# A two-layer decoder on one core: layer 0's self-attention stepped by two head pairs instead of one

## The chip, the cores and the metric

The kernel runs on one core of a Trainium2 chip, in one launch. A core has a matrix engine (TensorE, PE in the profile; its weight loads are shown apart as PEld), a vector engine (VectorE, DVE), a scalar engine (ScalarE, ACT), a general engine (GpSimd, POOL) and a queue engine for transfers (SyncE, SP). Each takes its own instructions in order, and they wait for one another by semaphores. TensorE writes to PSUM, which here is cut into eight tiles of 128 partitions by 512 float32 numbers, called banks below; the other operands lie in SBUF. The metric is the device time of one execution in microseconds, median of several executions.

## The reference, cut to what matters

The whole is a decoder of two layers over 16 sequences of 256 tokens with 128 features. The change lies in the first of six blocks, layer 0's self-attention: 16 heads of 64, a linear bias by distance, a causal mask, softmax. The blocks after it in layer 0 are a cross attention with a gate and a mixture of experts.

```python
def _L0_attn_ref(x, Wq, Wk, Wv, Wo, bo):
    q = (x @ Wq).reshape(b, n, H, DH)
    k = (x @ Wk).reshape(b, n, H, DH)
    v = (x @ Wv).reshape(b, n, H, DH)
    scores = jnp.einsum('bihd,bjhd->bhij', q, k) * scale + bias[None]
    scores = jnp.where(causal[None, None], scores, jnp.float32(-1e+30))
    attn = jax.nn.softmax(scores, axis=-1)
    out = jnp.einsum('bhij,bjhd->bihd', attn, v).reshape(b, n, H * DH)
    return out @ Wo + bo
...
x = x + _L0_attn_ref(_layernorm(x, axis=-1), ...)
x = x + _L0_xattn_ref(_layernorm(x, axis=-1), ctx_1024, ...)
x = x + _L0_ffn_ref(_layernorm(x, axis=-1), ...)
```

## The kernel before

**Units and stages.** The stage works on 128 units: a unit is a sequence `b` (16) and a pair of heads `pair` (8). A unit passes through these functions, each with its line in the profile:

- `scores` (L450): four matmuls, each head with 64 rows of the array, so that two heads run side by side; a head's causal scores are 128 and 256 columns wide, in a PSUM bank of its own (pool `ps_s`, four banks).
- `greatest` (L463, VectorE): adds the bias from a table, writes the scores to SBUF and keeps the row's extreme; two instructions a head.
- `exponentials` (L475, ScalarE): two a head, with the row sums.
- `scaled` (L484 a reciprocal on VectorE, L486 two products on GpSimd): divides by the sums.
- `flip` (L497, TensorE): three 128x128 transposes a head, in a bank of pool `ps_m`; `flipped` (L502, VectorE) copies them to SBUF.
- `values` (L512, TensorE): four matmuls, each with 64 columns of the array, into one tile of pool `ps_o` (one bank); `values_out` (L524, ScalarE) copies it to SBUF.

Besides these the stage has the projections: `qk_mm` (L395) and `qk_out` (L406, ScalarE) for two units at a time, `v_mm` (L412) and `v_out` (L421, VectorE), `y_mm` (L427) and `y_out` (L435) for the output of a sequence, and `turn` (L131) with `turned` (L385) for the normed input of a chunk of two sequences. All of them, like the transposes, take their banks in turn from the three of `ps_m`: a tile waits until the tile three before it has been read.

**The step.** A loop runs 134 steps; the order of TensorE, VectorE and ScalarE is that of the program, written out by hand, while GpSimd's and SyncE's order is left to the scheduler. At step i, scores are made for unit i, `greatest` and `exponentials` for unit i-1, `scaled` for unit i-2, `flip` for unit i-4 and `values` for unit i-5. On TensorE a step is: projections, scores, values, transposes, side pieces.

**Side pieces.** While the attention of later sequences runs, the cross attention, the norm and the router of earlier chunks are done in small pieces: `front_pieces(c)` is a list for chunk c of 512 tokens, and `plan` puts its k-th piece into step 16c+22+k. A piece has a part for TensorE, placed after the transposes, and a part for the others, placed last in the step. Those that the prediction speaks of: `root` (three small GpSimd instructions, L346 and L348), `p_centred` and `p_centred2` (a small VectorE instruction, then four on ScalarE, L365), `mm_turn` and `mm_turn2` (four transposes of the outcome, L131), `p_first` and `p_second` (the router's choice: some 18 small VectorE instructions), `mm_gate` (L689, L696; eight matmuls into two banks) with `p_gate` (L705, two tanh on ScalarE), and `p_put` (L790: two indirect DMAs issued by GpSimd, four times a chunk). The pieces of chunks 6 and 7 that are left over at the end run in the mixture of experts, one for each of its tiles.

```python
                for mm, _, _ in pieces:
                    mm()
                if at(0):
                    scores(at(0))
                if at(5):
                    values(at(5))
                if at(4):
                    flip(at(4), 0)
                    flip(at(4), 1)
                for mm, _ in more:
                    if mm:
                        mm()
```

The functions that the change touches, and what calls them:

Of the kernel before, what the change touches and what calls it, by code (L numbers as in the profile page):

```python
# [15 lines left out]
F32 = mybir.dt.float32  # L16
# [6 lines left out]
P = 128  # L23
B, N, D = 16, 256, 128
# [3 lines left out]
NCHUNK = T // CH  # L28
# [7 lines left out]
EARLY_C = 6  # L36
# [26 lines left out]
def kernel(ctx: ExitStack, tc: tile.TileContext, a: dict, out: bass.AP):  # L63
    nc = tc.nc
# [173 lines left out]
    with ExitStack() as ph:  # L238
        DH = 64
        NPAIR = H // 2  # L240
# [102 lines left out]
        def root(c, what, scale=1.0, shift=LN_EPS):  # L343

            ve = small.tile([P, TPC], F32, tag="ln_ve0", name=f"ve_{what}_{c}", bufs=2)
            nc.gpsimd.tensor_scalar(ve, lnv[what, c][:, :, 1], scale, shift, ALU.mult, ALU.add)  # L346
            rstd = small.tile([P, TPC], F32, tag="ln_rstdf", name=f"rstd_{what}_{c}", bufs=3)
            nc.gpsimd.tensor_tensor(rstd, ve, nhalf, ALU.pow)  # L348
            lnv["r", what, c] = rstd
# [153 lines left out]

        def values(u):
            b, pair = u
            po = o_of[u] = ps_o.tile([P, N], F32, tag="o", name=f"o0_{b}_{pair}")
            v = vals[b, pair // 4]
            for jt, c0 in ((0, 0), (1, P)):
                for h in (2 * pair, 2 * pair + 1):
                    rows = slice((h % 2) * DH, (h % 2 + 1) * DH)  # L510
                    pT = pT_of[b, h]
                    nc.tensor.matmul(  # L512
                        po[rows, c0:N], v[:, jt, h % 8 * DH : (h % 8 + 1) * DH],
                        pT[:, 0:N] if jt == 0 else pT[:, N:],
                        start=(jt == 0), stop=(jt == 1),
                    )
            for h in (2 * pair, 2 * pair + 1):
                del pT_of[b, h]

        def values_out(u):  # L520
            b, pair = u
            if pair == 0:
                oT[b] = qkvp.tile([P, NPAIR, N], F32, tag="oT", name=f"oT0_{b}", bufs=1)
            nc.scalar.copy(oT[b][:, pair, :], o_of.pop(u))  # L524

# [66 lines left out]
        def front_pieces(c):  # L594
# [239 lines left out]
            def p_sdown():  # L834
                nc.vector.tensor_tensor(x[c], x[c], g.pop("sy"), ALU.add)

            first_part = [
                (None, lambda: stats(c, 0, "x0")),
                (None, lambda: stats(c, 2, "x0")),
                (None, lambda: root(c, "x0")),  # L840
                (None, p_centred),
                (mm_turn, p_turned),
                (mm_scores, p_leaky),
# [9 lines left out]
                (None, lambda: stats(c, 0, "f0")),  # L853
                (None, lambda: stats(c, 2, "f0")),
                (None, p_root2),
                (None, p_centred2),
                (mm_turn2, p_turned2),
                (mm_logits, p_logits),
# [132 lines left out]
        with tc.manual_schedule(engines=ordered):  # L991
            for t0 in (0, 2):
                stats(0, t0)
            normed(0, nc.vector)
            bias_strips()
            biased(0)
            turn(0)
            turned(0)
            for g in range(2):
                for which in range(2):  # L1000
                    qk_mm(g, which)
                    qk_out(g, which)
            front_constants()

            units = [(b, p) for b in range(B) for p in range(NPAIR)]
            n = len(units)
            side = {}  # L1010

            def plan(first, pieces):
                for k, piece in enumerate(pieces):
                    side.setdefault(first + k, []).append(piece)

            plan(17, [(lambda h=h: ctx_turn(h), lambda h=h: ctx_turned(h)) for h in range(2)])
            for c in range(NCHUNK):
                first_step = 16 * c + 22
                plan(first_step, front_pieces(c))
                if c == EARLY_C - 1:  # L1020
                    plan(first_step + 24, early_pieces())
                if c == NCHUNK - 1:
                    plan(first_step + 25, late_pieces())
            steps = 8 * (B - 1) + 14
            for i in range(steps):
                b, p = divmod(i, NPAIR)

                def at(lag):
                    return units[i - lag] if 0 <= i - lag < n else None

                pieces = []
                if i + 4 < n:
                    key = ((i + 4) // 2, i % 2)
                    pieces.append((lambda: qk_mm(*key), None, lambda: qk_out(*key)))
                if b < B and p in (2, 3, 6, 7):
                    vkey = (b, p // 4, p % 2)
                    pieces.append((lambda: v_mm(*vkey), lambda: v_out(*vkey), None))
                if p == 5 and 1 <= b <= B:
                    pieces.append((lambda: y_mm(b - 1), lambda: y_out(b - 1), None))
                if p == 7 and b % 2 == 0 and b // 2 + 1 < NCHUNK:  # L1040
                    c = b // 2 + 1
                    pieces.append((lambda: turn(c), None, lambda: turned(c)))
                more = side.get(i, [])

                for mm, _, _ in pieces:
                    mm()
                if at(0):
                    scores(at(0))
                if at(5):
                    values(at(5))  # L1050
                if at(4):
                    flip(at(4), 0)
                    flip(at(4), 1)
                for mm, _ in more:
                    if mm:
                        mm()

                if at(1):
                    greatest(at(1), 0)
                if at(2):  # L1060
                    scaled(at(2), 0)
                for _, out_v, _ in pieces:
                    if out_v:
                        out_v()
                if at(2):
                    scaled(at(2), 1)
                if at(1):
                    greatest(at(1), 1)
                if at(4):
                    flipped(at(4), 0)  # L1070
                    flipped(at(4), 1)
                if b % 2 == 0 and b // 2 + 1 < NCHUNK:
                    if p in (1, 3):
                        stats(b // 2 + 1, p - 1)
                    elif p == 4:
                        normed(b // 2 + 1)
                    elif p == 6:
                        biased(b // 2 + 1)

                if at(1):  # L1080
                    exponentials(at(1), 0)
                for _, _, out_a in pieces:
                    if out_a:
                        out_a()
                if at(1):
                    exponentials(at(1), 1)
                if at(5):
                    values_out(at(5))
                for _, post in more:
                    post()  # L1090


    pending = []
# [1049 lines left out]
```

## Time and profile before

| | us |
|---|---|
| median of 3 runs | 1545.54 (1542.36 to 1545.73) |
| the profiled execution, its own time | 1542.13 |
| its span in the profile | 1540.4 |
| first scores of layer 0's self-attention start | 18.3 |
| last scores start | 625.3 |
| first expert tile's transposes start | 652.9 |

The span is the time between the first and the last instruction of the program in the profile. The stage that the change touches takes the first 653 us of it. From then on the mixture of experts and layer 1 follow, whose code is not touched. The profile names a group of instructions by line, engine, operation, output and inputs with the tile of the array for matmuls (64*128 is 64 rows by 128 columns), the shape, the count, the busy time and the mean, and the idle time of the engine in front of them with what ended it.

### The profile page before, as it was taken

To read this page: it belongs to the slowest core of one execution; us is meant where nothing else is said; L and a number is where in the kernel's file an instruction comes from. 1 tells how busy PE (TensorE), PEld (TensorE's weight loads), DVE (VectorE), ACT (ScalarE), POOL (GpSimd) and SP (SyncE) were. 2 spreads that over 40 slices of the span, in tenths; PEclk is the share of its full clock that TensorE was granted. 3 is DMA by queue.
4 is the path that set the end of the run, shared out by engine and by line. 5 is a ranking of instruction groups with operands and counts; after the bars stand their busy time and mean duration, and the time that the engine had idled before them with its cause. 6 is when DMAs were issued, how large, how long until landed. Compare 5 with 4: busy or idle time off the path is not lost.

```text
span 1540.4 us, 34885 instructions
## 1 busy us (share of the span) xinstructions
PE 1460.9 (95%) x11569; PEld 1066.0 (69%) x11569; DVE 1175.1 (76%) x4620; ACT 970.7 (63%) x2619; POOL 664.8 (43%) x1102
## 2 busy tenths in 40 slices
PE   7999999999999999899999899999999996899987
PEld 4676666666666666589999777777777663565564
DVE  6666666667676767687878679999999977888873
ACT  5666565656565656354333378888888874667762
POOL 7354646464747464554533311111111006657642
PEclk9999999999999999999999989999999997999999
DMA  7760000000000000468777200000000000112122
GB/s 219 247 204 1 1 14 3 9 8 5 12 1 15 2 15 1 133 181 242 222 233 235 98 15 8 15 16 8 15 1 2 2 1 1 29 42 64 36 59 53
DMA packets 76321, 95.01 MB, mean 62 GB/s; under 512 B 15936, under 2 KB 59200, under 8 KB 76144
## 3 DMA queue, kind: packets, MB, share of 16 engines
q1 hardware_dynamic: 61312, 45.59, 10.9%
q10 hardware_dynamic: 10512, 38.28, 7.8%
q0 software_dynamic: 4320, 8.92, 1.7%
q8 instruction: 94, 1.54, 0.4%
q14 instruction: 83, 0.68, 0.2%
HBM read 64.11 MB, written 28.65 MB: 60 GB/s over the span
## 4 chain that ended last, share of the span: by engine, by line
PE 80%; DVE 13%; ACT 4%; issue 2%; DMA 1%; POOL 1%; POOLq 0%; DVEq 0%; SPq 0%; ACTq 0%
PE t L1587 7%; PE pqk L395 7%; PE s L450 6%; PE o L512 6%; PE t L497 5%; PE s L1555 5%; PE g L1298 4%; PE y L427 4%; PE u L1298 4%; PE y L1316 4%; PE o L1602 4%; PE pv L412 3%; PE pqk L1468 3%; DVE p L1566 2%; PE yf L2012 2%
## 5 line engine op out<-in xcount | busy, mean ns | idle before, releaser
L475 ACT ACTIVATE p<-p,nm 128x128 f32<-128x128 f32 (+1 forms) x512 | 227.6, 446 | 183.7 <-DVE nm L463 168.3
L486 POOL TENSOR_SCALAR p<-p,rs 128x128 f32<-128x128 f32 (+1 forms) x512 | 212.4, 431 | 188.8 <-DVE rs L484 160.8
L1577 ACT ACTIVATE p<-p,nm 128x256 f32<-128x256 f32 x512 | 225.9, 509 | 38.3 <-DVE nm L1566 35.9
L502 DVE COPY pT<-t 128x384 f32<-128x384 f32 x256 | 130.8, 552 | 101.8 <-PE t L497 101.8
L1566 DVE CUSTOM_DVE_ANT_0 p<-s,strip 128x256 f32<-128x256 f32 x512 | 188.0, 419 | 18.2 <-PE s L1555 16.0
L463 DVE CUSTOM_DVE_ANT_0 p<-s,strip 128x128 f32<-128x128 f32 (+1 forms) x512 | 158.0, 346 | 1.6 <-PE s L450 1.6
L1587 PEld LDWEIGHTS t<-ident,p 128*128 128x128 f32 x1024 | 111.2, 142 | 48.6 <-issue 13.0
L1587 PE MATMUL t<-ident,p 128*128 128x128 f32 x1024 | 141.5, 282 | 1.2 <-DVE pT L1595 1.2
L1433 POOL TENSOR_SCALAR ve_a<-mv_a 128x2 f32<-128x2 f32 x16 | 3.7, 229 | 267.8 <-DVE mv_a L1428 267.7
L1326 POOL DMA_INDIRECT rows_out<-yr,to x71 | 68.5, 964 | 116.2 <-DVE yr L1325 107.8
L450 PE MATMUL s<-k,q 64*128 64x128 f32 (+1 forms) x1024 | 118.5, 350 | 0.0
L512 PE MATMUL o<-pT,v 128*64 128x256 f32 (+1 forms) x1024 | 112.3, 339 | 0.8 <-DVE pT L502 0.8
L497 PE MATMUL t<-ident,p 128*128 128x128 f32 x768 | 112.9, 282 | 0.2 <-ACT k L406 0.2
L450 PEld LDWEIGHTS s<-k,q 64*128 64x128 f32 x1024 | 67.1, 186 | 62.5 <-issue 56.6
L512 PEld LDWEIGHTS o<-pT,v 128*64 128x64 f32 x1024 | 62.7, 136 | 61.4 <-issue 25.2
L497 PEld LDWEIGHTS t<-ident,p 128*128 128x128 f32 x768 | 81.6, 141 | 23.3 <-issue 16.1
L475 ACT ACTIVATION_READ_ACCUMULATOR p<-p,nm 128x1 f32 x512 | 96.6, 189 | 0.0
L1306 ACT ACTIVATE gs<-gs 128x512 f32<-128x512 f32 x71 | 44.7, 630 | 77.8 <-DVE gs L1305 65.6
L1595 DVE COPY pT<-t 128x512 f32<-128x512 f32 x128 | 87.8, 687 | 5.4 <-PE t L1587 2.3
L1555 PE MATMUL s<-k,q 32*128 32x256 f32 x1024 | 86.6, 410 | 1.4 <-DVE nm L1566 1.3
L421 DVE COPY v<-pv 128x512 f32<-128x512 f32 x64 | 43.9, 686 | 50.7 <-PE pv L412 50.7
L790 POOL DMA_INDIRECT rows_in<-xn,slot_in x64 | 63.7, 995 | 35.7 <-DVE nm L463 20.4
(338 smaller groups left out, 3482.1 us busy)
## 6 DMA issues: line engine op xcount, KB each, us to landing
gu<-in_L_ffn_gate_up_w ACTq DMA_DIRECT2D x71, 512.0 KB
rows_in<-zero SPq DMA_DIRECT2D x131, 130.0 KB
spread<-wrows SPq DMA_DIRECT2D x16, 512.0 KB
xr<-rows_in SPq DMA_DIRECT2D x71, 65.0 KB
y<-rows_out SPq DMA_DIRECT2D x16, 256.0 KB
x<-in_x SPq DMA_DIRECT2D x8, 256.0 KB
out_x<-yo SPq DMA_DIRECT2D x16, 128.0 KB
rows_out<-yr,to POOLq DMA_INDIRECT x71, 3.7
```

What stands on the lines that cost most here:

```text
L450: nc.tensor.matmul(ps_of[b, h][:, cols], q[rows, u2, iq], k[rows, u2, 0:nk], start=True, stop=True,)
L463: nc.vector.tensor_tensor_reduce(out=pr[:, cols], in0=ps[:, cols], in1=strip[:, h, P : 2 * P] if it == 0 else strip[:, h, :], scale=1.0, s ...
L475: nc.scalar.activation(pr[:, cols], pr[:, cols], AF.Exp, bias=nm[:, it : it + 1], scale=-1.0, accum_out=sm[:, it : it + 1],)
L486: nc.gpsimd.tensor_scalar(pr[:, cols], pr[:, cols], rs[:, it : it + 1], 1.0, ALU.mult, ALU.mult)
L497: nc.tensor.transpose(ps[:, cols], pr[:, cols], ident)
L502: nc.vector.tensor_copy(pT_of[b, h], tp_of.pop((b, h)))
L512: nc.tensor.matmul(po[rows, c0:N], v[:, jt, h % 8 * DH : (h % 8 + 1) * DH], pT[:, 0:N] if jt == 0 else pT[:, N:], start=(jt == 0), stop=(j ...
L1298: nc.tensor.matmul(ps[:, f, :], gu[:, lo + f * P : lo + (f + 1) * P], xT, start=True, stop=True,)
L1555: nc.tensor.matmul(ps_of[b, h][:, it, :], q[rows, g, it * P : (it + 1) * P], k[rows, g, :], start=True, stop=True,)
L1566: nc.vector.tensor_tensor_reduce(out=pr[:, it, :], in0=ps[:, it, :], in1=strip1[:, h, (1 - it) * P : (1 - it) * P + N], scale=1.0, scalar= ...
L1577: nc.scalar.activation(pr[:, it, :], pr[:, it, :], AF.Exp, bias=nm[:, it : it + 1], scale=-1.0)
L1587: nc.tensor.transpose(ps[:, jt, it * P : (it + 1) * P], pr[:, it, jt * P : (jt + 1) * P], ident,)
```

## The change

A step of the loop handles two units (four heads), and there are 67 steps instead of 134. At double step j the scores, `greatest` and `exponentials` are those of units 2j and 2j+1, `scaled` and `flip` those of the two units before, `values` those of the two before these. On TensorE the order is: scores of two units, both projections `qk_mm`, the first step's side pieces, the other projections, values of two units, transposes of four heads, the second step's side pieces. `values` writes the two units into one tile of a bank, and `values_out` copies both at once. On ScalarE the copies `qk_out` stand between the exponentials of the four heads. The lists of side pieces get one or two empty places for the earlier chunks.

```diff
         def values(u):
             b, pair = u
-            po = o_of[u] = ps_o.tile([P, N], F32, tag="o", name=f"o0_{b}_{pair}")
+            if pair % 2 == 0:
+                o_of[b, pair // 2] = ps_o.tile([P, 2, N], F32, tag="o", name=f"o0_{b}_{pair}")
+            po = o_of[b, pair // 2][:, pair % 2, :]
...
-        def values_out(u):
-            b, pair = u
-            if pair == 0:
+        def values_out(b, two):
+            if two == 0:
                 oT[b] = qkvp.tile([P, NPAIR, N], F32, tag="oT", name=f"oT0_{b}", bufs=1)
-            nc.scalar.copy(oT[b][:, pair, :], o_of.pop(u))
+            nc.scalar.copy(oT[b][:, 2 * two : 2 * two + 2, :], o_of.pop((b, two)))
...
+            wait = [], [(None, lambda: None)]
             first_part = [
...
                 (None, lambda: root(c, "x0")),
+                *wait[c <= EARLY_C],
                 (None, p_centred),
...
                 (None, p_root2),
+                *wait[c < EARLY_C - 1],
                 (None, p_centred2),
...
-                    plan(first_step + 24, early_pieces())
+                    plan(first_step + 25, early_pieces())
...
-            for i in range(steps):
-                b, p = divmod(i, NPAIR)
+            for j in range(steps // 2):
+                b, p = divmod(2 * j, NPAIR)
...
+                heads = [(u, k) for u in at(0) for k in range(2)]
+                before_them = [(u, k) for u in at(1) for k in range(2)]
...
+                more = [side.get(i, []) for i in (2 * j, 2 * j + 1)]
...
+                for u in at(0):
+                    scores(u)
+                for mm, _, _ in pieces[0:2]:
+                    mm()
+                run(0, 0)
+                for mm, _, _ in pieces[2:]:
+                    mm()
+                for u in at(2):
+                    values(u)
+
+                for u, k in before_them:
+                    scaled(u, k)
+                outs = [out for _, _, out in pieces if out]
+                for n in range(4):
+                    if heads:
+                        greatest(*heads[n])
+                        exponentials(*heads[n])
+                    if n < 3 and outs:
+                        outs.pop(0)()
+                run(0, 1)
                 for _, out_v, _ in pieces:
                     if out_v:
                         out_v()
...
+                for u in at(2)[0:1]:
+                    values_out(u[0], u[1] // 2)
+
+                for u, k in before_them:
+                    flip(u, k)
+                run(1, 0)
+                for u, k in before_them:
+                    flipped(u, k)
...
+                run(1, 1)
```

Here `run(k, 0)` issues the TensorE parts of the k-th of the double step's two lists of side pieces, and `run(k, 1)` their other parts.

## The prediction

> **What bounds the kernel now.** First the busy times, the whole span and then a stretch in the middle of the stage.
>
> ```profile
> PE 1460.9 (95%) x11569; PEld 1066.0 (69%) x11569; DVE 1175.1 (76%) x4620; ACT 970.7 (63%) x2619; POOL 664.8 (43%) x1102
> ```
>
> ```profile
> 300.00:400.00 100.00, 98.66 (x702) 67.18 (x702) 70.58 (x328) 61.12 (x220) 62.00 (x112) 1.00 0.04 12
> ```
>
> In that row (PE, PEld, DVE, ACT, POOL, then the granted clock) TensorE has 98.66 of 100 us at full clock and nobody else more than 71: the stage lasts as long as TensorE's stream, plus what it waits. Next, TensorE in order of time (start, length with overlap, what):
>
> ```profile
> 302.31 0.87 PE L497 MATMUL t<-ident,p 128*128 128x128 f32 x6
> 303.02 1.03 PE L395 MATMUL pqk<-xnT,wk 128*128 128x256 f32 x4
> 303.89 1.02 PE L412 MATMUL pv<-wv,xnT 128*128 128x512 f32 x2
> 304.84 0.93 PE L450 MATMUL s<-k,q 64*128 64x128 f32 x8
> 305.69 0.87 PE L512 MATMUL o<-pT,v 128*64 128x256 f32 x8
> 306.50 0.88 PE L497 MATMUL t<-ident,p 128*128 128x128 f32 x6
> 307.21 1.02 PE L805 MATMUL sg<-xT,sgu 128*128 128x512 f32 x2
> ...
> 332.08 0.87 PE L497 MATMUL t<-ident,p 128*128 128x128 f32 x6
> 333.60 1.13 PE L395 MATMUL pqk<-xnT,wk 128*128 128x256 f32 x4 [0.64 <-ACT q L406]
> ```
>
> ```profile
> 355.63 0.88 PE L497 MATMUL t<-ident,p 128*128 128x128 f32 x6
> 357.22 0.66 PE L131 MATMUL tp_f<-ident,xn 128*128 128x128 f32 x4 [0.71 <-ACT k L406]
> ```
>
> Starts minus starts give true costs. pqk to pv: 512 columns in 0.86, so 0.214 for 128. The scores stream 384 columns, two heads side by side, 0.64, but take 0.85; values 0.64, but 0.80; six transposes at a pitch of 0.109, 0.65, but 0.71; pv takes 0.95 ahead of the scores and 0.86 elsewhere. So each change of the array's tile (64*128, 128*64, 128*128) costs: 0.095 at the end of the group before, and at the start of the new one 0.107 (scores), 0.05 (values), 0.06 (transposes); a projection after a 64-row or 64-column group starts 0.1 late (1.06 against 0.96). Both waits above return every 16 units: 1.52 and 1.59 from transposes to the next group against 0.71, together 1.7 a period of 81.0 us (sg at 307.21 and at 388.2).
>
> Last the stage's tail, with GpSimd's and VectorE's rows:
>
> ```profile
> 630.01 0.88 PE L497 MATMUL t<-ident,p 128*128 128x128 f32 x6
> 633.98 2.07 PE L817 MATMUL su<-xT,sgu 128*128 128x512 f32 x2 [3.08 <-DVE rs L669]
> ...
> 643.68 0.88 PE L497 MATMUL t<-ident,p 128*128 128x128 f32 x6
> ```
>
> ```profile
> 633.09 0.96 POOL L790 DMA_INDIRECT rows_in<-xn,slot_in  x1 [0.30 <-issue]
> 634.09 3.65 POOL L486 TENSOR_SCALAR p<-p,rs 128x128 f32<-128x128 f32 x8
> ```
>
> ```profile
> 644.27 1.02 DVE L502 COPY pT<-t 128x384 f32<-128x384 f32 x2 [3.79 <-PE t L497]
> ```
>
> After 3 us idle TensorE runs slowly: su took 2.07 against 1.02, clock 0.60 from 634 to 638. GpSimd had been issuing DMAs (one per 1.27 us) ahead of the softmax products.
>
> **The change part by part.** *Fewer tile changes.* A unit has three now: into scores 0.095+0.107, into values 0.095+0.05, into transposes 0.095+0.06: 0.50, 1.01 for two. A double step has four: 0.20, 0.15, 0.16, and scores to projections 0.095+0.1: 0.70. That saves 0.31 x 64 = 19.8. Of the side pieces, two (cw and sp, 64 columns) now stand between transposes and scores, where a change is paid anyway: 0.2 each, 2 x 6 chunks = 2.4.
>
> *Two waits.* Both were for a projection's bank, whose copy (L406) stood behind long side work on ScalarE. Now the copies stand among the exponentials, ahead of it: 1.7 x 6 = 10.2 gone; 0 if other banks are late there instead, which the next items count.
>
> *The fourth head's bank.* Four heads are transposed in a row into three banks; the fourth waits until VectorE has copied the first. From the tail's rows: the copy starts 0.59 after the first transpose (644.27-643.68), lasts 0.55, and a matmul follows some 0.08 later: 1.24 after the first transpose, where without a wait it would be 1.04. 0.20 x 64 = 12.8; nothing hides it, because scores stand behind it in TensorE's queue. Bounds 0.17 and 0.25: 11 to 16. [...] Were every copy waited for, it would be 4 x 0.475, the copies' pitch, less 4 x 0.33 of transposes: 0.6 a double step, 38 in all; the rows show three banks running ahead, so I keep 0.20.
>
> *Shorter distance from softmax to transposes.* It was two steps (9 us); now GpSimd's products come in the same double step. A clock of one, from the first score: scores end at 1.5, projections at 3.3, values 1.43 later, so transposes start at 4.8 at the earliest, and later where pv, y or side matmuls stand before them. VectorE ends the last copies at 0.8, then four reciprocals; GpSimd needs 0.82 a head: 1.1 to 4.4. Hidden by 0.4 us or more, if GpSimd is free. ScalarE: first exponential at 1.35, 0.89 a head, 0.48 a projection copy, the first of them not before 2.65: ends at 6.3. Four kinds of double step, once per period each, miss this clock:
> - Two `root`s: the compiled order of GpSimd puts them (1.1 + 2 x 0.28) ahead of the products, after two pairs of statistics (0.81 each) on VectorE; the products run from 3.4 to 6.7, the last transposes want theirs by 6.05. 0.55.
> - Two centrings: 2 x 1.55 on ScalarE (four L365 took 1.55) from 6.3 to 9.4, and `mm_turn` wants the second at 8.6 (it had a whole step). 0.9.
> - `p_second`: 2.4 of small instructions on VectorE, then two v copies of 0.61, stand ahead of the copies L502; the v banks come free at 7.2 and 7.9, the second and third head want them at 6.9 and 7.6, and the first copy starts only then. 0.6.
> - The gate: four banks in a row; projections and tanh free them 0.13 and 0.22 late. 0.35.
>
> Sum 2.4 x 6 = 14.4. None of them has a row of its own before: bounds 0 (each piece hidden) and twice that, 29. I take the worked clocks.
>
> *Tail.* GpSimd's compiled order has all eight DMAs of chunk 5 (8 x 1.27 = 10.2) ahead of the last four heads' products. From the step of the last two units on: matmuls 21.5, end 33.2 us later, so 11.7 lost; before, from 621.4 to 652.3 with 23.5 of matmuls, 7.4 lost. +4.3, between -2 and +8.
>
> *At nothing:* the 512-column copy of values (one of some 0.57 for two of 0.36; ScalarE idles 39%); one piece of chunk 6 that moves into the experts' tiles (VectorE alone, under TensorE's stream); SyncE's queue keeps its order and its transfers end before they are wanted. Without that cover: 1 us at most.
>
> Sum: -19.8-2.4-10.2+12.8+14.4+4.3 = -0.9. On the profiled execution's 1542.13: 1541.2; on the median of the runs, 3.4 higher, 1544.6. I say 1543.
>
> **Rivals.** *The waits of the special steps are hidden* (ScalarE and VectorE come to them earlier than my clocks): without 14.4 and 4.3 the sum is -19.6, about 1524. For it: both have 30 to 39% idle. Against: their queues are in order and the late work stands ahead by the program. Chance 0.20.
>
> *GpSimd becomes late* (slower). Seven DMAs (8.9 us) stand between the products of two double steps, and in later chunks mix and norm (7 us) ahead of the next. By my clock products end 0.8 us before their transposes want them. If each GpSimd piece is 10% longer than its row, that cover is gone and two double steps a period lose some 2 us each: 24 more, about 1567. It decides from 0.8 us on. For it: this is the shortest cover in the stage, and the tail's rows show just such a queue. Against: 62 of 100 us busy. Chance 0.17.
>
> *It does nothing*: the order compiled for TensorE shows eight score matmuls in a row, so tile changes do go. Only if a change costs nothing beyond its first would the time stay. Chance 0.03.
>
> **How the numbers follow.** My case, that new waits eat the saving, has 0.60, its own range 1533 to 1556. With bounds: low -19.8-2.4-10.2+11+5+2 = -14, 1529; high -22.2-5+16+22+8 = +19, 1562. That alone would leave out both rivals, 0.37, so the low end goes on to take in the faster one: 1521 to 1562, with some 0.18 left out, most of it the slower rival. This kernel's measurement tells 0.3%, 4.6 us. My case splits 0.20, 0.18, 0.22; with the rivals faster 0.40, same 0.21, slower 0.39.
>
> **What would show it.** Eight scores at 1.48 and eight values at 1.43 confirm the tile changes; a wait of 0.2 for VectorE's copy (L502) in front of the fourth head's transposes in each double step; a period near 80.6; a wait of 5 us near the end. Wrong if the period is under 79 (hidden waits) or over 83, with TensorE waiting for GpSimd's L486.

## The result, and the profile after

The changed kernel takes 1544.50 us (median of 12 runs, 1539.05 to 1552.34), the kernel before 1544.93 us beside it (12 runs, 1539.49 to 1550.91): a ratio of 1.0002, with a 95% interval from 0.9986 to 1.0018. Measured again on another occasion the ratio is 1.0004 (0.9987 to 1.0022). There is no difference that this measurement can tell. The profiled execution took 1547.82 us, its span is 1546.1.

That is not because nothing happened. Cut into four parts by the starts of TensorE's rows, with the second traces of both kernels beside the first, in us:

| part | before | before_again | after | after_again |
|---|---|---|---|---|
| start to first scores | 18.30 | 18.71 | 17.31 | 16.91 |
| first scores to first expert transpose (`xTr`) | 634.65 | 634.77 | 629.72 | 629.48 |
| first to last expert transpose | 211.91 | 211.89 | 219.50 | 218.10 |
| from there to the end of the span | 675.56 | 677.79 | 679.58 | 678.16 |
| one period of 16 units (`sg` to `sg`) | 81.03 | 81.04 | 79.92 | 79.88 |

The attention stage became 4.9 to 5.3 us shorter; the experts' part, whose code was not touched, became 6.2 to 7.6 us longer. In these two pairs the first scores start 1.0 and 1.8 us earlier, but in the traces of the other double-step kernels below they start between 17.2 and 18.4, so no gain is shown there. The last part is 2.2 us longer in the mean of two traces, as much as the two traces of the kernel before differ.

In three of the four sets of experiments below the kernel before itself took 1566 to 1568 us instead of 1545, and every double-step kernel traced there shows a stall that no other trace shows (last section), so times are compared only within a set, and TensorE's rows only in stretches without the stall.

The busy times and the stretch in the middle of the stage, for the kernel after:

```profile
PE 1458.2 (94%) x11569; PEld 1087.6 (70%) x11569; DVE 1176.0 (76%) x4620; ACT 965.2 (62%) x2555; POOL 659.5 (43%) x1102
```

```profile
300.00:400.00 100.00, 98.33 (x705) 70.09 (x703) 72.51 (x346) 62.78 (x220) 57.84 (x107) 1.00 0.04 11
```

TensorE is still busy for 98 of 100 us at full clock: the stage is still as long as TensorE's stream. Both waits of before for projection banks are gone. This is the list of what TensorE waited for over four periods (line, what it waited for, us in total, times, longest), first before, then after:

```profile
PE tp_f L131 <- ACT k L406: 2.9, 4, 0.7
PE pqk L395 <- ACT q L406: 2.5, 4, 0.6
```

```profile
PE t L497 <- DVE v L421: 1.3, 4, 0.3
```

5.4 us of waits became 1.3, and the one that is left is the router's choice (`p_second`), whose `v` copy stands ahead on VectorE. TensorE in order of time, for the kernel after:

```profile
301.24 1.52 PE L514 MATMUL o<-pT,v 128*64 128x256 f32 x16
302.69 0.55 PE L497 MATMUL t<-ident,p 128*128 128x128 f32 x3
303.56 1.58 PE L497 MATMUL t<-ident,p 128*128 128x128 f32 x9 [0.32 <-DVE v L421]
...
305.56 1.58 PE L450 MATMUL s<-k,q 64*128 64x128 f32 x16
307.07 1.13 PE L395 MATMUL pqk<-xnT,wq 128*128 128x256 f32 x4
...
309.33 1.52 PE L514 MATMUL o<-pT,v 128*64 128x256 f32 x16
310.79 1.81 PE L497 MATMUL t<-ident,p 128*128 128x128 f32 x12
312.45 1.13 PE L806 MATMUL sg<-xT,sgu 128*128 128x512 f32 x2
```

Starts minus starts: eight scores take 1.51 (305.56 to 307.07) where two groups of four took 1.71, eight values 1.46 (309.33 to 310.79) where they took 1.60. Twelve transposes take 1.66 (310.79 to 312.45), and 1.74 where scores follow, where two groups of six took 1.42. The group is printed without a wait: the fourth head's pause, about a quarter of a microsecond, lies inside it, and only the instructions' own starts show it.

The stage's tail, TensorE and then GpSimd:

```profile
613.51 1.58 PE L450 MATMUL s<-k,q 64*128 64x128 f32 x16
...
620.74 1.58 PE L497 MATMUL t<-ident,p 128*128 128x128 f32 x9 [1.05 <-DVE v L421]
...
625.27 0.61 PE L664 MATMUL sm<-half_of,ex 128*128 128x2 f32 x4 [1.51 <-ACT ex L659]
...
630.73 3.55 PE L497 MATMUL t<-ident,p 128*128 128x128 f32 x12 [2.85 <-POOL p L486]
634.08 1.91 PE L818 MATMUL su<-xT,sgu 128*128 128x512 f32 x2
```

```profile
629.30 0.96 POOL L791 DMA_INDIRECT rows_in<-xn,slot_in  x1 [0.30 <-issue]
630.30 3.24 POOL L486 TENSOR_SCALAR p<-p,rs 128x128 f32<-128x128 f32 x8
```

The last transposes wait 2.85 us for GpSimd's products, which stand behind the last of the chunk's DMAs. With the waits of 1.51 and 1.05 and one of 0.34 that is 5.75 us, and the transposes at 630.73 run at half speed (clock 0.50 from 626.6 to 636.8).

The experts' part: what TensorE waits for, from the first to the last expert transpose, before and then after:

```profile
PE g L1298 <- ACT xTs L1270: 1.3, 3, 0.6
PE u L1298 <- DVE hT L1310: 1.1, 1, 1.1
PE xTr L1266 <- DVE x L435: 0.5, 1, 0.5
```

```profile
PE g L1311 <- ACT xTs L1283: 4.1, 5, 2.6
PE u L1311 <- DVE hT L1323: 1.7, 2, 1.1
PE sm L664 <- ACT ex L659: 1.2, 1, 1.2
...
```

2.9 us became 7.7 (the line left out is the 0.5 for `x` again, and one of 0.2 follows): 4.8 of the 7.6. Two places hold most of it. TensorE in order of time, first the rows of before, then those of after that hold both places:

```profile
684.07 1.06 PE L1298 MATMUL u<-xTs,gu 128*128 128x128 f32 x8
684.96 1.02 PE L805 MATMUL sg<-xT,sgu 128*128 128x512 f32 x2
685.82 0.51 PE L663 MATMUL sm<-half_of,ex 128*128 128x2 f32 x4
```

```profile
682.46 0.61 PE L664 MATMUL sm<-half_of,ex 128*128 128x2 f32 x4 [1.24 <-ACT ex L659]
685.85 1.02 PE L806 MATMUL sg<-xT,sgu 128*128 128x512 f32 x2
...
707.54 1.18 PE L1311 MATMUL g<-xTs,gu 128*128 128x128 f32 x8 [2.56 <-ACT xTs L1283]
708.53 1.89 PE L1311 MATMUL u<-xTs,gu 128*128 128x128 f32 x8
```

Before, chunk 6's `sg` stood in the same tile as chunk 7's `sm` and ahead of it: its microsecond covered the exponential that `sm` needs. With an empty place more in chunk 6's list, `sg` comes a tile later, and `sm` waits bare. The second place is the wait of 2.56 at 707.54, after which `u` takes 1.89 instead of 1.06: the clock was 0.51 from 708.5 to 711.9. On ScalarE the copy that it waits for stands behind an issue of expert weights, which itself waited, by the profile, for a transfer of layer 1's weights (`wq_u`) that SyncE had issued:

```profile
706.57 0.35 ACTq L1272 DMA_DIRECT2D gu<-in_L_ffn_gate_up_w  x1
707.02 0.46 ACT L1283 ACTIVATE xTs<-xTr,bet,gam 128x128 f32<-128x128 f32 x1 [5.28 <-DMA wq_u<-in_L_xattn_wq]
```

In the second trace of the changed kernel the sum of waits is 7.7 again, the longest 1.6, with no half clock here. So 4.8 of the 6.2 to 7.6 us are waits in both traces and about 1.7 (half of 3.4 us) are the clock in the first; some 1.2 are not accounted for.

### The profile page after: what moved, and what is told of

It reads as the page before. It is cut to its first block, busy times and chain, and to the rows that moved or that the text cites. A ratio compares the mean times of both kernels' runs of the same rounds, so it can differ in the third digit from the quotient of the medians.

```text
span 1546.1 us, 34991 instructions
## 1 busy us (share of the span) xinstructions
PE 1458.2 (94%) x11569; PEld 1087.6 (70%) x11569; DVE 1176.0 (76%) x4620; ACT 965.2 (62%) x2555; POOL 659.5 (43%) x1102
## 4 chain that ended last, share of the span: by engine, by line
PE 72%; DVE 14%; ACT 5%; issue 4%; POOL 3%; DMA 1%; ACTq 0%; POOLq 0%; SPq 0%; DVEq 0%
PE t L1600 8%; PE pqk L395 6%; PE s L1568 5%; PE s L450 5%; PE t L497 5%; PE o L514 4%; PE o L1615 4%; PE y L427 4%; PE g L1311 3%; PE y L1329 3%; PE u L1311 3%; PE pqk L1481 3%; PE pv L412 2%; PE yf L2025 2%; PE tx L1879 2%
## 5 line engine op out<-in xcount | busy, mean ns | idle before, releaser
L486 POOL TENSOR_SCALAR p<-p,rs 128x128 f32<-128x128 f32 (+1 forms) x512 | 209.2, 430 | 108.4 <-DVE rs L484 107.0
L502 DVE COPY pT<-t 128x384 f32<-128x384 f32 x256 | 125.7, 550 | 77.3 <-PE t L497 77.1
L463 DVE CUSTOM_DVE_ANT_0 p<-s,strip 128x128 f32<-128x128 f32 (+1 forms) x512 | 146.9, 352 | 11.3 <-PE s L450 9.8
L1600 PE MATMUL t<-ident,p 128*128 128x128 f32 x1024 | 142.4, 283 | 1.2 <-DVE pT L1608 1.2
L497 PE MATMUL t<-ident,p 128*128 128x128 f32 x768 | 115.9, 283 | 12.3 <-POOL p L486 3.2
L450 PE MATMUL s<-k,q 64*128 64x128 f32 (+1 forms) x1024 | 101.2, 337 | 0.0
L514 PE MATMUL o<-pT,v 128*64 128x256 f32 (+1 forms) x1024 | 97.8, 333 | 0.0
L1319 ACT ACTIVATE gs<-gs 128x512 f32<-128x512 f32 x71 | 44.7, 630 | 79.9 <-DVE gs L1318 66.8
L450 PEld LDWEIGHTS s<-k,q 64*128 64x128 f32 x1024 | 72.6, 187 | 14.4 <-issue 9.4
L1311 PE MATMUL g<-xTs,gu 128*128 128x128 f32 x568 | 75.7, 276 | 4.2 <-ACT xTs L1283 4.1
```

The source lines that it names most:

```text
L450: nc.tensor.matmul(ps_of[b, h][:, cols], q[rows, u2, iq], k[rows, u2, 0:nk], start=True, stop=True,)
L463: nc.vector.tensor_tensor_reduce(out=pr[:, cols], in0=ps[:, cols], in1=strip[:, h, P : 2 * P] if it == 0 else strip[:, h, :], scale=1.0, s ...
L486: nc.gpsimd.tensor_scalar(pr[:, cols], pr[:, cols], rs[:, it : it + 1], 1.0, ALU.mult, ALU.mult)
L497: nc.tensor.transpose(ps[:, cols], pr[:, cols], ident)
L502: nc.vector.tensor_copy(pT_of[b, h], tp_of.pop((b, h)))
L514: nc.tensor.matmul(po[rows, c0:N], v[:, jt, h % 8 * DH : (h % 8 + 1) * DH], pT[:, 0:N] if jt == 0 else pT[:, N:], start=(jt == 0), stop=(j ...
```

## The experiments

**Scores apart again (split_scores, split_again).** The cost of a tile change on its own: the scores of the two units with a projection between them, all else as in the changed kernel.

```diff
-                for u in at(0):
+                n_qk = 2 if 2 * j + 4 < len(units) else 0
+                for k, u in enumerate(at(0)):
                     scores(u)
-                for mm, _, _ in pieces[0:2]:
-                    mm()
+                    for mm, _, _ in pieces[k : min(k + 1, n_qk)]:
+                        mm()
                 run(0, 0)
-                for mm, _, _ in pieces[2:]:
+                for mm, _, _ in pieces[n_qk:]:
                     mm()
```

> The changed kernel, but with each unit's scores followed by one projection instead of both units' scores together. Theory 1 (the forecast's: every change of the array's tile costs TensorE time that nothing hides): two more changes per double step, scores to projection 0.095 and 0.1, projection to scores 0.095 and 0.107, 0.40 x 64 = 25 us more, 1570, ratio 1.017; two groups of eight scores at 0.85 instead of one of sixteen at 1.51. Theory 2 (the changes lie under other waits): within 5 us of 1544.5, since the wait for the fourth bank or for the softmax shrinks by as much.

Measured 1594.13 us against 1568.35 of the kernel before, ratio 1.0154 (1.0131 to 1.0178); with the stall in it, this says nothing of a tile change. It was run once more:

> The split of the scores once more, for a chip without the unnamed stall. Theory 1 (a change of the array's tile costs TensorE about 0.1 at each end and nothing hides it): two more changes per double step, 0.40 x 64 = 25 us over the changed kernel's 1544.8, 1570, ratio 1.016; the period rises from 79.9 by 3.2. Theory 2 (the changes lie under other waits): within 5 us of 1544.8.

1589.93 against 1566.16, 1.014 (1.010 to 1.0179), the stall again. The rows can be read all the same. TensorE in order of time, in the second run:

```profile
194.13 0.93 PE L450 MATMUL s<-k,q 64*128 64x128 f32 x8
194.98 1.13 PE L395 MATMUL pqk<-xnT,wq 128*128 128x256 f32 x4
196.04 0.93 PE L450 MATMUL s<-k,q 64*128 64x128 f32 x8
```

Four scores take 0.85 or 0.86 again and each projection behind them 1.06. Per period scores and `pqk` cost 13.69 + 16.32 where they cost 12.09 + 14.74: 3.19 more, 0.40 for each of eight double steps, as the prediction's prices say (two entries at 0.2). From the first scores to the fifth `y`, a stretch of 23 double steps with no stall, the split kernel takes 198.54 us and the changed one 191.29, 7.25 more: scores and `pqk` take 9.2 more, again 0.40 a double step, and `pv`, transposes and `tp_x` 1.9 less. Tile changes do cost what the rows of before showed.

**A fourth bank for the transposes (bank4).** The first of four heads takes its bank from the scores' pool.

```diff
-            ps = tp_of[b, h] = ps_m.tile([P, 3 * P], F32, tag="m", name=f"t0_{b}_{h}")
+            if h % 4 == 0:
+                ps = ps_s.tile([P, 4 * P], F32, tag="s", name=f"t0_{b}_{h}")[:, 0 : 3 * P]
+            else:
+                ps = ps_m.tile([P, 3 * P], F32, tag="m", name=f"t0_{b}_{h}")
+            tp_of[b, h] = ps
```

> The changed kernel, but the first of four heads is transposed into one of the four banks of the scores, so that the four heads have four banks. Theory 1 (the forecast's third term): in each double step the pitch before the fourth head's transposes is 0.36 instead of 0.11, with the one behind it 0.28 lost; it goes, 0.28 x 64 = 17.7 us less, 1527, ratio 0.989, and the sixteen-step transposes take 1.46. Theory 2 (VectorE's copies are the bound, so the wait only moves): the scores' fourth bank is now wanted before its copy (L502) has ended, TensorE waits there instead, less than 5 us come off, 1540 or more.

1586.93 against 1568.35, 1.0112 (1.0091 to 1.0132): the least of the four of this set, and all four have the stall. What the bank brings is read below, in the kernel that holds this edit and no stall.

**Chunk 6 without its empty place (slot6, slot6_again).** The edit takes back the part of the change that moved chunk 6's pieces one tile on in the experts.

```diff
-                *wait[c <= EARLY_C],
+                *wait[c < EARLY_C],
```

> The changed kernel, but chunk 6 without its empty slot, so that its last pieces keep their old place beside the experts' tiles. Theory 1 (giveback at the experts): in the changed kernel GpSimd issues chunk 6's eight put DMAs from 689.3 to 699.3 and two rows_out after them, so chunk 7's mix1 (L711) runs at 701.88 although its tanh ended at 695.63; VectorE (L716) then holds back xTs and TensorE waits 2.56 us at 707.5 and runs at half clock for some 4 us. One tile (3 us) earlier, mix1 follows its tanh at once, the wait and the slow clock go: 4 to 5 us less, 1540, ratio to before 0.997. Theory 2 (the difference between 647 and 712 is that of two executions): no wait goes, 1544.5, ratio 1.000.

1591.86 against 1568.35, 1.0145 (1.0122 to 1.0168), with the stall. Run again, without the stall:

> The changed kernel without chunk 6's empty slot, measured beside the changed kernel itself. Theory 1 (giveback at the experts): GpSimd's mix1 of chunk 7 (L711) follows its tanh at once, the wait of 2.56 us before a tile's g and the half clock behind it go, 4 to 5 us under the changed kernel in the same call. Theory 2 (the difference between 647 and 712 is that of two executions): the same as the changed kernel.

1545.20 against 1546.15, 0.9993 (0.9973 to 1.0013). The experts' part came down to 215.56 us, with neither the wait of 1.24 nor that at 707; but the stage went up to 632.51. (The expectations lay the wait at 707 to GpSimd's late `mix1`; in the rows of the changed kernel it is ScalarE's issue of weights, shown above, that ends it.) TensorE in order of time shows where:

```profile
598.48 0.66 PE L131 MATMUL tp_x<-ident,xn 128*128 128x128 f32 x4 [1.43 <-ACT q L406]
599.84 1.12 PE L412 MATMUL pv<-wv,xnT 128*128 128x512 f32 x2 [0.70 <-ACT k L406]
601.75 1.12 PE L412 MATMUL pv<-wv,xnT 128*128 128x512 f32 x2 [0.78 <-DVE v L421]
...
657.10 1.81 PE L1311 MATMUL g<-xTs,gu 128*128 128x128 f32 x8 [2.23 <-ACT xTs L1283]
```

Without the empty place chunk 6's first centring falls into the same double step as chunk 5's second, eight ScalarE instructions (1.65 + 1.64 us) in one go, and two banks wait behind the copies that stand after them, a third behind a `v` copy: 2.9 us, which is what the stage lost. The wait of 2.23 at 657.10 comes from GpSimd: a small mask for layer 1 is made there behind a memset of 3.51 us, and VectorE, in its compiled order, has the mask's reduction (L1163) ahead of the first tile's gate, behind which ScalarE's next copy for TensorE stands. GpSimd, then VectorE:

```profile
649.35 3.51 POOL L1148 MEMSET vbd<- 128x4096 f32 x1 [2.67 <-PE y L427]
```

```profile
654.57 0.18 DVE L1163 TENSOR_REDUCE rmask<-hmask 128x4 f32<-128x16 f32 x1 [4.01 <-DMA xr<-rows_in]
```

The place is a trade: 2.5 to 3.9 us won among the experts, 2.8 to 3.0 lost in the stage.

**The two kernels themselves again, and both edits together (before_again, after_again, bank4_slot6).** These belong to one set with slot6_again, in which the kernel before took 1546.15 (25 runs) and no trace has the stall.

> The kernel before, for a trace on the chip of this call. In the chip of the last call every kernel showed one stall per period that the earlier traces lack: ScalarE (or VectorE) waits up to 5.5 us for a releaser that the profile can't name, while GpSimd issues eight put DMAs, and TensorE then runs at half clock for 3 to 7 us. Theory 1 (the chip does it, to every kernel): a call on the same chip shows it here too, 1568; on another chip it is absent, 1545. Theory 2 (only the double steps provoke it): no such stall here on any chip.

> The changed kernel, beside the kernel before on the same chip. Theory 1 (the stall belongs to the chip): without it, period 79.9 and ratio 1.000; with it, period 87 and ratio 1.01 to 1.02. Theory 2 (the experiments' edits provoked it): period 79.9 on any chip.

> The run before, and with the first of four heads transposed into a bank of the scores. Theory 1 (the wait for the fourth bank, 0.28 x 64 = 17.7 us, goes): 17 us under the run before; the period falls by 2.2. Theory 2 (VectorE's copies are the bound, the wait only moves to the scores' fourth bank): less than 5 us.

The kernel before, again: 1544.90 (one run). The changed one: 1544.82, 1.0004 (0.9987 to 1.0022). Both edits together: 1538.30 us, ratio 0.9958 (0.9935 to 0.9981), 6.9 us under slot6_again: the only version here that is measurably faster than the kernel before (of its ten runs only the longest, 1543.84, lies above the shortest of the changed kernel's ten, 1543.56). Its stage takes 626.61 us (632.51 in slot6_again), its experts' part 215.44. TensorE in order of time, in two double steps of it:

```profile
331.97 1.53 PE L501 MATMUL t<-ident,p 128*128 128x128 f32 x12
333.43 1.58 PE L450 MATMUL s<-k,q 64*128 64x128 f32 x16
...
346.85 2.51 PE L501 MATMUL t<-ident,p 128*128 128x128 f32 x12
349.29 1.58 PE L450 MATMUL s<-k,q 64*128 64x128 f32 x16
```

Where scores follow, twelve transposes take 1.46 instead of 1.74: the 0.28 of the fourth head are gone. But the saving is only 5.9 us, not 0.28 x 64 = 17.9, and the period falls by 0.28 (79.91 to 79.63), not by 2.2: in a full period only two of the eight double steps gain the 0.28. Where another group that takes one of the three banks follows (`sg`, `sy`, `tp_f`), transposes to that group take the same 1.66 or 1.75 as without the further bank; ahead of `cw` they gain 0.08; ahead of `pos` they take 2.36 instead of 2.31, and in the double step of the roots, at 346.85, 2.44 instead of 2.17. 3.9 of the 5.9 us lie ahead of the first `sg` (at 228), where fewer side pieces stand. So the size of the pause was read rightly from the rows; what a further bank returns is a third of it over the stage, and an eighth in a full period. The experts' part starts 6.0 us earlier than in slot6_again and is as long (215.44 and 215.56), so it does not wait for something that comes at a fixed time.

**The v copies ahead of the router's choice (vout_first).**

```diff
-                run(0, 1)
+                own = any(mm for mm, _ in more[0])
+                if own:
+                    run(0, 1)
                 for _, out_v, _ in pieces:
                     if out_v:
                         out_v()
+                if not own:
+                    run(0, 1)
```

> The changed kernel, but with the v copies (L421) ahead of a side piece that has no matmul of its own (p_second). Theory 1 (the forecast's special step): the transposes of that double step take 1.74 instead of 2.30 from their start to the next group, 0.56 x 6 = 3.4 us less, 1541, ratio 0.998. Theory 2: p_second's 2.4 us now delay the copies L502 behind it or the positions' matmul, and the wait comes back there: 1544.5.

1590.58 against 1568.35, 1.0136 (1.0112 to 1.016), with the stall; and a miss in the rows too. TensorE, then VectorE:

```profile
223.74 1.20 PE L497 MATMUL t<-ident,p 128*128 128x128 f32 x9
226.09 0.52 PE L497 MATMUL t<-ident,p 128*128 128x128 f32 x3 [1.15 <-DVE pT L502]
```

```profile
225.40 1.94 DVE L502 COPY pT<-t 128x384 f32<-128x384 f32 x4
```

The copies now wait for `pv`, the router's small instructions begin only after them, and the copies of the transposes start at 225.40: the fourth head waits 1.15, and the group takes 2.72 us instead of 2.30. In this double step, whichever stands first on VectorE, the other is late.

**Chunk 6 kept in place without losing its empty place (realign), and the puts of chunk 5 later (late_puts_h).** realign joins two pieces of chunk 6's list, so that the empty place shifts nothing behind it:

```diff
-                (None, lambda: stats(c, 0, "f0")),
-                (None, lambda: stats(c, 2, "f0")),
+                *([
+                    (None, lambda: (stats(c, 0, "f0"), stats(c, 2, "f0"))),
+                ] if c == EARLY_C else [
+                    (None, lambda: stats(c, 0, "f0")),
+                    (None, lambda: stats(c, 2, "f0")),
+                ]),
```

> The changed kernel with chunk 6's empty slot kept, but its two pairs of second statistics in one piece, so that from there on its pieces keep their old place beside the experts' tiles. Theory 1 (in the changed kernel the shifted pieces cost the experts' part 6.2 to 7.6 us, of which a late rmask 0.7): the attention stage keeps its 629.5 us from first scores to first expert transpose, the experts' part falls from 218.1 or 219.5 to about 213, 5 to 6 us less, 1539, ratio 0.997. Theory 2 (any place of these pieces costs as much, as the run without the slot suggests, which gave back in the stage what it gained): 1545.

late_puts_h gives chunk 5 two empty places ahead of its puts, so that they stand behind the last products on GpSimd, and makes the mask among the constants at the start:

```diff
                 (None, p_second),
+                *wait[c == EARLY_C - 1],
+                *wait[c == EARLY_C - 1],
                 (mm_pos, p_pos),
...
-    hmask = lpool.tile([P, H], F32, tag="hmask", name="hmask")
```

> The changed kernel with chunk 5's token positions two slots later, so that its eight put DMAs stand behind the last four heads' products on GpSimd, and with the head masks built at the start. Theory 1 (the forecast's tail: products behind eight puts): the wait of 3.0 us before the last transposes, most of the 1.0 and 1.2 waits ahead of it and some 5 us lost to half clock behind them go, the first expert transpose comes at 640 instead of 646.4, 1539, ratio 0.996. Theory 2 (the puts then end at 634 and the rows that the experts fetch are late by as much): the first expert transpose waits for its rows, 1545 or more.

realign: 1584.49 against 1566.16, 1.0103 (1.0061 to 1.0145). late_puts_h: 1581.21, 1.0088 (1.0054 to 1.0122). Both have the stall, and their intervals overlap. In realign's trace the wait of `sm` among the experts is gone. It is there, 1.23 to 1.25 us long, in all seven traces of kernels in which chunk 6 is shifted, and in none of the five in which it is not (slot6, slot6_again, bank4_slot6, realign, combined), nor in the two of the kernel before: this much is shown. late_puts_h removed the wait of 2.85 before the last transposes (0.19 is left), but TensorE waits at the next place:

```profile
656.21 1.20 PE L497 MATMUL t<-ident,p 128*128 128x128 f32 x6 [0.19 <-DVE rs L678]
...
679.47 1.86 PE L1313 MATMUL g<-xTs,gu 128*128 128x128 f32 x7 [7.66 <-ACT xTs L1285]
```

```profile
672.33 6.51 ACTq L1274 DMA_DIRECT2D gu<-in_L_ffn_gate_up_w  x3
678.96 0.81 ACT L1285 ACTIVATE xTs<-xTr,bet,gam 128x128 f32<-128x128 f32 x2 [12.77 <-DMA xr<-rows_in]
```

ScalarE issues three transfers of expert weights (6.51 us) ahead of the first tile's copy. By the profile they wait for SyncE's fetches of the tokens' rows (`xr`), the first of which is issued at 668.26, 4.7 us after the start of the last put, as in the changed kernel (634.20 after 629.30): the expectation's second theory. In the changed kernel the weight issues end at 646.5, under the tail. What the tail's wait costs therefore can't be taken out alone.

**All of them (combined).** The changed kernel with bank4, realign and the early mask.

> The changed kernel with three edits at once: the first of four heads transposed into a bank of the scores, chunk 6's two second statistics in one piece (its slot in the stage kept, its place beside the experts' tiles as before the change), and the head masks built at the start. Theory 1 (the edits' gains add: 5.9 in the stage for the fourth bank, 6.2 in the experts' part for the old place of the pieces and an rmask that waits for nothing long): where the stall of the put DMAs is absent, 1545 - 5.9 - 6.2 = 1533, ratio 0.993, with about 624 us from first scores to first expert transpose and 212 for the experts' part. Theory 2 (ScalarE's seven weight DMAs, which end at 645.8 in the changed kernel, hold the first expert tile): the stage cannot end before some 642, the experts' part starts with a wait for xTs, 1537. Where the stall is present, the ratio is about 1.01 by both.

1582.80 against 1566.38, 1.0097 (1.0072 to 1.0122), with the stall. What realign and this version take without it was not measured, so whether anything under bank4_slot6's 1538.3 is within reach stays open.

## Why the prediction held, and where it was wrong

The forecast of 1543 us held: 1544.5. "New waits eat the saving" is what happened, but only in part where the forecast put them: 5 us of the saving outlived the stage and were given back behind it. That these two errors, of opposite sign and like size, met is luck. Per period of 16 units, starts minus starts, mean of four periods:

| TensorE's groups | before | after | difference |
|---|---|---|---|
| scores | 13.69 | 12.09 | -1.61 |
| values | 12.83 | 11.61 | -1.21 |
| projections `pqk` and `pv` | 22.76 | 21.99 | -0.77 |
| transposes of heads (with their waits) | 13.45 | 14.78 | +1.33 |
| `tp_x` | 0.47 | 0.95 | +0.48 |
| all others | 17.88 | 18.49 | +0.61 |
| period | 81.08 | 79.91 | -1.17 |

- *Tile changes (-19.8).* Right in price: eight scores, at 1.51 instead of the 1.48 forecast, save 0.201 (worked out: 0.202), eight values, at 1.46 for 1.43, save 0.152 (0.145), and the split kernel gives back 0.40 for two more changes. The -2.4 of the side pieces doesn't show in `cw` and `sp` themselves, 0.58 and 0.59 as before, but in part in the groups beside them: before, the transposes ahead of `cw` took 0.81 (0.71 elsewhere) and the first matmul of the projections behind `cw` and `sp` 0.32 (0.22 elsewhere); after, no projection stands behind them, and the transposes take the same 1.74 ahead of `cw` as ahead of scores. Against it `sg` takes 1.06 ahead of `sp`, where `su` took 0.95.
- *Two waits (-10.2).* Right: both are gone from the list of waits, and the list has nothing in their place but 0.3 a period.
- *The fourth head's bank (+12.8).* Mis-sized: too small, and outside its bounds of 11 to 16. The fourth head's first transpose comes 0.36 after the transpose before it, instead of 0.109, and the next is 0.03 late too: 0.28 a double step, 17.9 in 64. It is too short to be printed as a wait, so the expected line does not appear. The 0.28 lies between my 0.20 and the 0.6 of every copy waited for; and bank4_slot6 shows that "nothing hides it" is right only where scores follow: elsewhere a further bank moves the wait to the next group.
- *Four special double steps (+14.4).* All four are there: roots 0.45 (0.55), centrings 0.48 (0.9), `p_second` 0.57 (0.6), gate 0.26 (0.35: `pre` 3.44 instead of 3.28, and `pv` behind it 0.10 longer than elsewhere, which may be a tile change). Together 1.76 a period, 10.6 in six; the centrings were mis-sized.
- *Tail (+4.3).* Right: from the last double step's scores (613.51) to the end of the last `y` (646.5) 33.0 us pass, where 33.2 were worked out, and the waits come to 5.75, where 5 were named.
- *The stage as a whole.* Predicted -0.9, measured -4.9 to -5.3, and a period of 79.9 instead of 80.6. The terms above that were too high and too low nearly cancel. Part of what is left is in the projections: in before, the first matmul of eight projection groups a period takes 0.30 to 0.32 instead of 0.22, six of them behind a side piece (`ax`, `cw`, `sm`, `sp`, `pos`, `pre`) and two behind a wait; in the changed kernel, apart from the first group behind the scores, which the sum had priced, only the one behind `pre` starts so late. The sum had counted two of the six. On the other side `sy` and `sg`, now ahead of a group with another tile, take 0.2 more each. The rest was not taken apart. The bounds of the range took 5 and 22 for the special double steps, 2 for the tail and -5 for the two waits, where the working had named 0, 29, -2 and 0; what was measured lies inside both.
- *"At nothing: ... one piece of chunk 6 that moves into the experts' tiles".* This is the step that failed most. The prediction looked at the piece that moves in (VectorE alone) and priced it at 1 us at most; but all of chunk 6's pieces behind it move one tile on, against chunk 7's, which stay. The experts' part became 6.2 to 7.6 us longer. The `sm` wait follows the shift through all traces. The late `xTs` is not explained by the shift alone: in the trace it stands behind an issue of weights that waited for another transfer, and in the second trace it is 1.6 instead of 2.56. slot6_again shows that undoing the shift returns 2.5 to 3.9 us of the 6.2 to 7.6; the remaining 3.7 are about what the late mask's wait of 2.23 and the half clock behind it (half of 3.4) cost there, but no run without the stall took that mask away alone. So of the 6.2 to 7.6 the 1.24 of `sm` are shown to come from the shift, and the rest is argued.

Of the rivals, neither the hidden waits (1524) nor the late GpSimd (1567) came about. The special steps did cost 1.76 a period; and in the regular double steps TensorE's transposes have no pause but the fourth head's, with GpSimd busy for 57.8 of 100 us. Its products come late only in the double step of the roots (pauses of 0.2 to 0.5 us, the 0.45 above) and in the tail, both as forecast. That the change does nothing is refuted by the stage.

## What to carry to other kernels

Grouping work of one array tile saves what starts minus starts say (here 0.2 for scores and 0.15 for values per double step), but each group in a row wants as many banks as it has outputs before the first is emptied (here the fourth of four heads on three banks waited 0.28 a double step); price the wait, and where the next group in line wants a bank too, expect one more bank to return only a part of it (here 5.9 of 17.9 us). A list of work that is moved by one place is not one piece moved: lay each of its pieces beside the neighbours it will then have, in each queue, above all beyond the stage that is being edited. A total that does not change can hold two differences of 5 to 7 us; cut the span at rows that both kernels share before believing it.

## What the runs showed of the hardware

**A stall beside scattered transfers.** In three sets of runs, where the kernel before took 1566 to 1568 us, the double-step kernels took 1581 to 1594, 0.9 to 1.5% more than it. In seven of their eight traces the lists of waits have ScalarE and VectorE waiting for "remote", the profile's word for a release that it can't put down to an instruction: four or five times a trace in the stage for `q` or `k` (up to 5.5 us long in slot6), and up to 7.3 us behind the stage (`xTs` in realign). Of combined there is the list of TensorE's own waits, with the same 1.7 us ahead of `t` as bank4's. In slot6 the matmul group that is waited for has ended, by TensorE's rows. ScalarE, TensorE and GpSimd there:

```profile
329.34 0.60 ACT L406 ACTIVATE q<-pqk 128x512 f32<-128x512 f32 x1 [5.16 <-remote]
```

```profile
323.09 1.13 PE L395 MATMUL pqk<-xnT,wq 128*128 128x256 f32 x4
...
329.99 0.70 PE L690 MATMUL pre<-wcat,xnT 128*128 128x256 f32 x2 [4.05 <-ACT q L406]
```

```profile
326.94 0.95 POOL L791 DMA_INDIRECT rows_in<-xn,slot_in  x1 [0.30 <-issue]
```

The projection ends at 324.2, its reader starts at 329.34. The eight puts of the chunk run from 314.7 to 327.9; the stall ends 2.4 us after the start of the eighth, and 2.4 us is the median that the profile gives for a put's way from issue to landing in the changed kernel. TensorE then runs at clock 0.50 for 6.8 us (330.6 to 337.4). From one `y` to the next a half period with puts takes 49 to 51 us in slot6 instead of 42.6, one without puts 37.3 as in the traces without the stall. That the puts delay the release of TensorE's groups is argued from this, not shown: no run had them removed. The chip alone does not decide it: the same chip showed the stall in one set (split_again, realign, late_puts_h) and not in another (after_again and those beside it), against the first theory of before_again and after_again. The changed kernel itself and the kernel before were not traced where the stall is, so neither why the kernel before loses less nor what the changed one takes there is known.

**Half clock in steps.** In the traces of before and after, the stretches at clock 0.5, but for the last of each, last 3.4 us or a multiple of it (3.4 from 633.8 in before; 10.2 from 626.6, 6.8 from 1206.9 and 20.5 from 1275.1 in after). The wait of 2.56 before 707.54 was followed by one of 3.4 (clock 0.51 from 708.5 to 711.9), the wait of 2.23 before 657.10 in slot6_again by about as much (0.93 from 640 to 660, 0.98 from 660 to 680: together 1.8 us of full clock lost), the waits of 1.6 and less in the same place of the changed kernel's second trace by none (1.00 from 640 to 720). Whether a short wait costs its own length or, by my estimate, 1.7 us more (half of 3.4), three waits are too few to tell.
